# A copy on ScalarE between the values' bank and VectorE's transposition, and one order for all slots, in a fused two-layer cross-attention kernel

## The chip, the cores and the metric

The kernel runs on one core of a Trainium2 chip. The metric is device time in microseconds (us) of one execution; lower is better. The engines are called as the profile calls them: PE is TensorE's matmul, PEld its weight load, DVE is VectorE, ACT is ScalarE, POOL is GpSimd, SP is SyncE, which issues most of the DMAs.

## The reference, cut to what matters

Two cross-attention layers follow each other. x has 32 batches of 256 rows and 320 channels; each batch has a context of 77 rows of 512 channels. There are 20 heads of 16 channels. In the first layer the context is cut into the text (77 rows) and three further parts, which are empty here, since there are 77 rows in all; the same holds for the second layer. What is left in each layer is

```
q = heads(x @ Wq);  k = heads(ctx @ Wk);  v = heads(ctx @ Wv)     # 20 heads of 16
s = q @ k^T / sqrt(16)                                            # 256 x 77 for each head
p = softmax(s);  o = merge(p @ v)
x = o @ Wo + bias + x                                             # input of the next layer
```

All of it is float32.

## The kernel before, in words

x stands turned in SBUF, channels on the partitions. Two batches are handled together, as a pair; a **unit** is one pair in one layer, so there are 16 pairs x 2 layers = 32 units. The 40 (batch, head) products of a unit are worked in five **groups**, g = 0 to 4, each with four pairs of heads side by side in the four 32-row or 32-column tiles of PE's array.

For a group the steps are these.

- `maxima` (L491 on): PE computes the scores once in float32 into four PSUM banks (`psm`, L500), and DVE takes the maximum of each row (L512). `turn` (DVE, then DMAs) brings a unit's maxima into the place where the scores step reads them.
- `scores` (L545 on): PE computes the scores turned, keys on the partitions, into four banks (`pss`): first minus the maximum (L550), then the product from split halves (L558). ACT takes four exponentials of 77x512 (L564, tile `pT`).
- `products` (L566 on, called by `values`): PE multiplies with the values, and with a column of ones for the sums, into one bank `po` of 128x512 (L578).
- `divide` (L587, called by `values`): DVE turns the bank in 32x32 blocks into SBUF (`turned`, L590) and takes the reciprocal of the sums (`inv`, L594); POOL multiplies (`normal`, L599).
- `turn_back` (L610): DVE turns `normal` back into the unit's output tile `oT` (L613).

When all five groups of a unit are in `oT`, `outputs_and_queries` (L388) multiplies with Wo (`psy`) and, interleaved with it, makes the queries of another unit (`psq`). Within it `main_channels` and `rest_main` read groups 0 to 3 of `oT`; `last_channels` and `rest_last` read group 4, and they come behind. Then DVE adds bias and residual (`x`, L620) and ACT copies the queries out of PSUM (L418, L421). `keys` makes `psk` (ACT copies it, POOL masks it), `vals` makes `psv` (ACT copies it into a stage, DMAs place it).

PSUM is one pool of eight banks; `po`, `pss`, `psm`, `psk`, `psv`, `psy` and `psq` all draw from it in turn, so that the bank that a step wants next is the one taken eight allocations ago.

The order of all instructions is written out by hand (`tc.manual_schedule()`): each engine runs its instructions in the order in which the program issues them. The main loop at the end walks over **slots**; `at(slot, where, step)` puts a step into a slot, and within a slot the steps go by their `where`. Slots from -10 to 0 start the kernel, slots 1 to 134 carry the units. `slot_of` gives the slot of a group's scores; its values come one slot later, and its `turn_back` two slots later (`"turn back"`), for g = 4 at the end of the values' own slot (`"back"`).

Before the change a slot is called heavy when the columns put down for it with `at(..., columns)` exceed 10 x 256, and two orders are in use:

```
        if slot > 0 and work_of[slot] > 10 * S:
            order = ("load", "scores", "turn back", "maxima") + rest
        else:
            order = ("load", "maxima", "turn back", "scores") + rest
```

with rest = ("values", "rest", "back", "turn", "split", "full", "last"). In every slot the values come behind the scores.

A unit takes four slots (or five where its number is a multiple of 4). The first of them is the large one: the scores of groups 0 and 1 (eight exponentials; in units 4, 8, ..., 28 only group 0, four exponentials, and a step of maxima), the values of the unit before's group 4, its `"back"`, and `outputs_and_queries` of the unit before. Then come slots of 3.5 to 6.2 us with one group's scores, one step of maxima, one or two groups' values, and some of keys and vals.

Of the kernel before, what the change touches and what calls it, by code (L numbers as in the profile page):

```python
# [59 lines left out]
HEADS, HD = 20, 16  # L60
# [35 lines left out]
def xattn_kernel(ctx: ExitStack, tc: tile.TileContext, xT, cT, cP, weights, outT):  # L96
# [24 lines left out]

    def load_context(u):
        p = units[u][0]
        c_sb = cs[u] = io.tile([P, NKA, NB * L], F32, tag="c", name=f"c_{u}", bufs=3)
        nc.sync.dma_start(out=c_sb, in_=cP[:, p])


# [23 lines left out]

    ones = const.tile([P, P], F32, name="ones")
    nc.vector.memset(ones, 1.0)
    ident = const.tile([P, P], F32, name="ident")
    make_identity(nc, ident)


# [160 lines left out]
    def keys(u, t):  # L318
        p, layer = units[u]
        w, c_sb = w_sb[layer], cs[u]  # L320
        if t == 0:
            st[u]["kr"] = work.tile([P, NG, L], F32, tag="kR", name=f"kR_{u}", bufs=2)
        kR = st[u]["kr"]
        ps = bank(f"psk_{u}_{t}")
        for kc in range(NKA):
            by_columns(
                ps[:, 0 : 2 * L],
                w["k"][:, kc, t * P : (t + 1) * P],
                c_sb[:, kc, :],
                start=(kc == 0),  # L330
                stop=(kc == NKA - 1),
            )
        nc.scalar.copy(kR[:, 2 * t : 2 * t + 2].rearrange("p g k -> p (g k)"), ps[:, 0 : 2 * L])
        mask_keys(u, t)

    def keys_rest(u):

        p, layer = units[u]
        w, c_sb = w_sb[layer], cs[u]
        ps = bank(f"psk_{u}_2")  # L340
        for kc in range(NKA):
            for i in range(4):
                b, m = 1 - i // 2, i % 2
                nc.tensor.matmul(  # L344
                    ps[32 * i : 32 * i + 32, 0:L],
                    w["k"][:, kc, 2 * P + 32 * m : 2 * P + 32 * m + 32],
                    c_sb[:, kc, b * L : (b + 1) * L],
                    start=(kc == 0),
                    stop=(kc == NKA - 1),
                )  # L350
        nc.scalar.copy(st[u]["kr"][:, 4], ps[:, 0:L])
        mask_keys(u, 2)
# [35 lines left out]
    def outputs_and_queries(u, uq):  # L388

        w, wq, o, x = w_sb[units[u][1]], w_sb[units[uq][1]], st[u]["o"], xs[units[uq][0]]  # L390
        q0 = new_queries(uq)
        y = [[bank(f"psy_{u}_{t}_{b}") for b in range(NB)] for t in range(2)]
        main_channels(y, w["o"], o, start=True, stop=False)
        y2 = bank(f"psy_{u}_2")
        rest_main(y2, w["o"], o, start=True, stop=False)


        q2 = bank(f"psq_{uq}_2")
        q = [[bank(f"psq_{uq}_{t}_{b}") for b in range(NB)] for t in range(2)]
# [12 lines left out]
        for g in range(4):  # L412
            add(u, g, y[g // 2][g % 2])
        add(u, 4, y2)
        store(u)

        rest_main(q2, wq["q"], x, start=False, stop=True, swap=1)
        nc.scalar.copy(of_group(q0, 4), q2[:, 0:S])  # L418
        main_channels(q, wq["q"], x, start=False, stop=True)
        for g in range(4):  # L420
            nc.scalar.copy(of_group(q0, g), q[g // 2][g % 2][:, 0:S])  # L421
# [165 lines left out]
    def divide(u, g, po):  # L587

        turned = work.tile([P, 2 * (S + HD)], F32, tag="turned", name=f"turned_{u}_{g}", bufs=2)
        nc.vector.transpose(turned[:, 0 : 2 * S], po)  # L590

        sums = turned[:, HD : 2 * S - HD].rearrange("p (e n) -> p e n", e=2)[:, :, 0 : S - HD : 32]
        inv = work.tile([P, 2, S // 32], F32, tag="inv", name=f"inv_{u}_{g}", bufs=2)
        nc.vector.reciprocal(inv, sums)  # L594

        outs = turned.rearrange("p (e n) -> p e n", e=2)[:, :, 0:S]
        outs = outs.rearrange("p e (q r) -> p e q r", r=32)[:, :, :, 0:HD]
        normal = work.tile([P, S // 32, 2, HD], F32, tag="normal", name=f"normal_{u}_{g}", bufs=2)
        nc.gpsimd.tensor_tensor(  # L599
            normal.rearrange("p q e d -> p e q d"),  # L600
            outs,
            inv.unsqueeze(3).broadcast_to([P, 2, S // 32, HD]),
            ALU.mult,
        )
        return normal
# [47 lines left out]

    place = {}

    work_of = {}

    def at(slot, where, step, columns=0):

        place.setdefault((slot, where), []).append(step)  # L660
        work_of[slot] = work_of.get(slot, 0) + columns

    def start(u):

# [18 lines left out]
    for u, (p, layer) in enumerate(units):  # L683

        s = start(u - 2)
        if layer == 0 and u > 0:
            at(s - 5 - (u == 1), "load", lambda p=p: load_x(p))
        if u > 0:
            at(s - 4, "load", lambda u=u: load_context(u))
        if u > 1:  # L690
            k = (0, 1, 2) if u == 2 else (s - 2, s - 1, s + 1)
            at(k[0], "rest", lambda u=u: keys(u, 0), 8 * 2 * L)
            at(k[1], "rest", lambda u=u: keys(u, 1), 8 * 2 * L)
            at(k[2], "rest", lambda u=u: keys_rest(u), 8 * L)
        paired = u > 2 and u - 3 not in late
        if paired:
            at(s, "full", lambda u=u: outputs_and_queries(u - 3, u), 50 * S)
        elif u > 1:
            at(s, "last", lambda u=u: queries(u), 25 * S)
        if u > 1:  # L700
            at(s + 2, "split", lambda u=u: split_keys(u))
            at(start(u - 1), "load", lambda u=u: spread_keys(u))
            for i in range(3):
                at(start(u - 1) + i - 1, "split", lambda u=u, i=i: split_queries(u, i))
                at(start(u - 1) + i, "load", lambda u=u, i=i: spread_queries(u, i))
        need = range(p * NB * L // P, ((p + 1) * NB * L - 1) // P + 1)
        new = [i for i in need if i >= made[layer]]
        made[layer] += len(new)
        first = (-6, -2)[u] if u < 2 else start(u - 1) + 1
        slots = {}  # L710
        for k, i in enumerate(new):
            at(first - 3 - (u == 0) + k, "load", lambda layer=layer, i=i: load_chunk(layer, i))
            if i in few:
                slots[i] = first
                at(first, "full", lambda layer=layer, i=i: vals_of_few(layer, i), 8 * 96)
                continue
            for h in range(2):
                slots[i] = first + (0 if u < 2 else k if len(new) > 1 else h)
                at(slots[i], "full", lambda layer=layer, i=i, h=h: vals(layer, i, h), 4 * C)
        for i in need:  # L720
            at(slots.get(i, first), "full", lambda u=u, i=i: place_vals(u, i))
        for g in range(NG):
            slot = slot_of(u, g)
            at(slot, "scores", lambda u=u, g=g: scores(u, g))
            at(slot + 1, "values", lambda u=u, g=g: values(u, g), 4 * S)
            if g < 4:
                at(slot + 2, "turn back", lambda u=u, g=g: turn_back(u, g))
            else:
                at(slot + 1, "back", lambda u=u, g=g: turn_back(u, g))
        if u == NU - 1:  # L730
            at(end, "full", lambda u=u: finish(u), 20 * S)
            at(end, "last", lambda u=u: finish_rest(u))
        if u in late:
            for t in range(2):
                at(late[u][t], "full", lambda u=u, t=t: finish(u, (t,)), 10 * S)
            at(late[u][2], "rest", lambda u=u: finish_rest(u), 5 * S)
            at(max(late[u]), "last", lambda u=u: store(u))


# [59 lines left out]

    rest = ("values", "rest", "back", "turn", "split", "full", "last")  # L800
    for slot in range(min(s for s, _ in place), max(s for s, _ in place) + 1):
        if slot > 0 and work_of[slot] > 10 * S:
            order = ("load", "scores", "turn back", "maxima") + rest
        else:
            order = ("load", "maxima", "turn back", "scores") + rest
        for where in order:
            for step in place.get((slot, where), ()):
                step()
# [98 lines left out]
```

## Time and profile before

| what | value |
|---|---|
| median of 3 runs (lowest to highest) | 938.5 us (937.83 to 941.53) |
| profiled execution, its own time | 937.7 us |
| its span in the profile | 935.9 us |
| granted TensorE clock | 0.999 |
| PE busy | 924.1 us, 99% of the span |
| PEld busy | 634.5 us, 68% |
| DVE busy | 572.4 us, 61% |
| ACT busy | 435.9 us, 47% |
| POOL busy | 413.6 us, 44% |

The profiled execution's own time lies 1.8 us above its span and 0.8 us below the median of the runs. Busy shares are of the whole span; a matmul's end is modelled, and matmuls overlap, so a busy PE is not a PE without waits: the waits are seen in how long a slot takes from its first matmul to the next slot's first.

### The profile page before, as it was taken

Reading aid. Unit: us, or ns where it says so; the run is one execution under the profiler, and the core shown is the slowest. Engines: PE = TensorE matmul, PEld = TensorE weight load, DVE = VectorE, ACT = ScalarE, POOL = GpSimd, SP = SyncE. Lnnn points to the kernel's source line nnn. Section 1 sums busy time; section 2 is a strip of 40 time slices with the busy share of each in tenths; the row PEclk is TensorE's granted clock in tenths of the full one; section 3 lists DMA queues with packets and bytes.
Section 4 is the critical chain, followed back from the end, with each engine's and each line's share of the span. In section 5 each row is a group of like instructions: output and inputs, shape, how many; then the busy total and the mean of one; then the engine's idle time right before and its main releaser. Section 6 shows DMA issues by size and latency. Waiting matters only on the chain.

```text
span 935.9 us, 48848 instructions
## 1 busy us (share of the span) xinstructions
PE 924.1 (99%) x21582; PEld 634.5 (68%) x21582; DVE 572.4 (61%) x1324; ACT 435.9 (47%) x975; POOL 413.6 (44%) x614
## 2 busy tenths in 40 slices
PE   9999999999999999999999999999999999999998
PEld 7667766777666777666766667766677766676654
DVE  4485656656566665656556566665467554776575
ACT  2355443554435553454534545434454445444562
POOL 4464334543345543345434455343554335553431
PEclk9999999999999999999999999999999999999999
DMA  6675245352453624545145452354434543344342
GB/s 242 218 225 163 84 132 171 96 191 81 150 178 103 203 67 148 165 142 189 52 140 171 125 184 82 123 171 162 160 95 118 165 158 115 94 141 126 119 137 98
DMA packets 114740, 133.03 MB, mean 142 GB/s; under 512 B 47012, under 2 KB 76004, under 8 KB 114530
## 3 DMA queue, kind: packets, MB, share of 16 engines
q1 hardware_dynamic: 113666, 127.42, 42.8%
q8 instruction: 170, 2.79, 1.3%
q10 hardware_dynamic: 864, 2.49, 0.7%
q14 instruction: 40, 0.33, 0.1%
HBM read 35.39 MB, written 10.49 MB: 49 GB/s over the span
## 4 chain that ended last, share of the span: by engine, by line
PE 88%; DVE 8%; DMA 2%; issue 1%; SPq 0%; POOL 0%; ACT 0%; ACTq 0%; POOLq 0%
PE psq L203 15%; PE psy L203 15%; PE po L578 14%; PE psm L500 8%; PE pss L558 8%; PE psv L203 7%; PE psk L203 6%; PE pss L550 5%; DVE m L512 4%; PE psy L237 4%; PE psq L237 4%; DVE turned L590 2%; PE psk L344 1%; DVE maxes L533 1%; DMA qs<-halves 1%
## 5 line engine op out<-in xcount | busy, mean ns | idle before, releaser
L564 ACT ACTIVATE pT<-pss 77x512 f32<-77x512 f32 x640 | 327.3, 594 | 125.9 <-PE pss L558 120.1
L512 DVE TENSOR_REDUCE m<-psm 128x6 f32<-128x462 f32 (+2 forms) x512 | 247.4, 549 | 208.6 <-PE psm L500 208.1
L599 POOL TENSOR_TENSOR normal<-turned,inv 128x256 f32<-128x256 f32 x160 | 99.5, 622 | 472.5 <-DVE inv L594 452.8
L578 PE MATMUL po<-pT,v 77*32 77x256 f32 x2560 | 165.9, 384 | 4.7 <-DVE m L512 2.7
L203 PE MATMUL psy<-oT,w 128*32 128x256 f32 (+1 forms) x3072 | 164.4, 379 | 0.0
L203 PE MATMUL psq<-x,w 128*32 128x256 f32 (+1 forms) x3072 | 155.6, 380 | 0.5 <-DMA w<-in_w_dram 0.3
L203 PEld LDWEIGHTS psy<-oT,w 128*32 128x32 f32 (+1 forms) x3072 | 88.3, 108 | 63.4 <-issue 14.4
L590 DVE STREAM_TRANSPOSE turned<-po 128x512 f32<-128x512 f32 x160 | 110.3, 689 | 25.6 <-PE po L578 25.5
L203 PEld LDWEIGHTS psq<-x,w 128*32 128x32 f32 (+1 forms) x3072 | 86.0, 109 | 57.7 <-DVE x L620 4.5
L274 POOL TENSOR_SCALAR kT<-kR,masks 128x154 f32<-128x154 f32 x186 | 113.6, 621 | 0.0
L578 PEld LDWEIGHTS po<-pT,v 77*32 77x32 f32 x2560 | 69.6, 109 | 63.4 <-ACT pT L564 18.6
L279 POOL TENSOR_TENSOR halves<-q,halves 128x512 fp32r<-128x512 f32 (+1 forms) x96 | 106.9, 1114 | 8.0
L500 PE MATMUL psm<-kT,q 32*128 32x154 f32 x2560 | 109.4, 296 | 0.0
L558 PE MATMUL pss<-qs,kS 32*77 32x256 f32 x2560 | 106.3, 275 | 0.0
L613 DVE STREAM_TRANSPOSE oT<-normal 128x256 f32<-128x256 f32 x160 | 67.4, 429 | 55.9 <-POOL normal L599 55.9
L620 DVE SCALAR_TENSOR_TENSOR x<-psy,w,x 128x256 f32<-128x256 f32 x160 | 68.4, 476 | 50.7 <-PE psy L203 49.4
L500 PEld LDWEIGHTS psm<-kT,q 32*128 32x128 f32 x2560 | 90.6, 183 | 12.9 <-issue 9.7
L558 PEld LDWEIGHTS pss<-qs,kS 32*77 32x77 f32 x2560 | 88.9, 141 | 10.9
L203 PE MATMUL psv<-w,cv 128*32 128x160 f32 x2432 | 93.2, 299 | 0.2 <-DVE m L512 0.2
L418 ACT COPY q<-psq 128x256 f32<-128x256 f32 x28 | 10.4, 372 | 169.6 <-PE psq L237 169.6
L550 PE MATMUL pss<-max_rows,less 32*77 32x512 f32 x640 | 80.5, 451 | 1.6 <-ACT stage L442 1.6
L203 PEld LDWEIGHTS psv<-w,cv 128*32 128x32 f32 x2432 | 76.8, 110 | 5.2 <-DVE m L512 0.7
(46 smaller groups left out, 725.1 us busy)
## 6 DMA issues: line engine op xcount, KB each, us to landing
qs<-halves SPq DMA_DIRECT2D x256, 128.0 KB
kS<-k_halves SPq DMA_DIRECT2D x128, 192.5 KB
c<-in_cP_dram SPq DMA_DIRECT2D x32, 308.0 KB
cv<-in_cT_dram SPq DMA_DIRECT2D x38, 256.0 KB
out_dram<-x SPq DMA_DIRECT2D x15, 640.0 KB
x<-in_xT_dram SPq DMA_DIRECT2D x14, 640.0 KB
qs<-halves SPq DMA_DIRECT2D x128, 64.0 KB
v<-stage SPq DMA_DIRECT2D x26, 192.5 KB
```

The source lines that it names most:

```text
L203: nc.tensor.matmul(out[m : m + 32], lhsT[:, m : m + 32], rhs, **flags)
L237: nc.tensor.matmul(ps[o : o + 32, 0:S], lhsT, rhs, **flags)
L274: engine.tensor_scalar_mul(kT[:, e], kR[:, groups], masks[:, e : e + 1])
L279: engine.tensor_tensor(low, x, high.bitcast(F32), ALU.subtract)
L500: nc.tensor.matmul(ps[j][:, i * 2 * L : (i + 1) * 2 * L], q[r, c * P : (c + 1) * P], kT[r, :, g % 2, :], start=True, stop=True,)
L512: nc.vector.tensor_reduce(st[u]["m"].rearrange("p e h j -> p h e j")[:, first : first + n, :, j], ps[j][:, at * 2 * L : (at + n) * 2 * L]. ...
L550: nc.tensor.matmul(ps[j][:L], less[r, g % 4, :], max_rows[u % 2][r, g // 4], start=True, stop=False)
L558: nc.tensor.matmul(ps[j][:L, e * S : (e + 1) * S], st[u]["ks"][r, e, g, half, :], q[r, :], start=False, stop=(half == 1 and e == 1),)
L564: nc.scalar.activation(st[u]["p", g][j][:L], ps[j][:L], AF.Exp, scale=SCALE)
L578: nc.tensor.matmul(po[o : o + 32, e * S : (e + 1) * S], vpad[:L, b, pair, e].rearrange("p a d -> p (a d)"), pT[j][:L, e * S : (e + 1) * S] ...
L590: nc.vector.transpose(turned[:, 0 : 2 * S], po)
L599: nc.gpsimd.tensor_tensor(normal.rearrange("p q e d -> p e q d"), outs, inv.unsqueeze(3).broadcast_to([P, 2, S // 32, HD]), ALU.mult,)
```

## The change

Three things change.

- In `divide`, ACT copies the bank `po` (128x512) into a new SBUF tile `whole`, and DVE turns `whole` instead of the bank. `normal` no longer has a tile of its own; it is written over the first half of `whole`.
- To make room, the context tile `c` has two buffers instead of three, and the identity matrix lies in a buffer of `turned`.
- The columns given to `at` and the sum `work_of` are gone; every slot behind slot 0 has the order with the scores ahead and the maxima behind `"turn back"`.

```diff
     def load_context(u):
-        c_sb = cs[u] = io.tile([P, NKA, NB * L], F32, tag="c", name=f"c_{u}", bufs=3)
+        c_sb = cs[u] = io.tile([P, NKA, NB * L], F32, tag="c", name=f"c_{u}", bufs=2)
...
-    ident = const.tile([P, P], F32, name="ident")
+    ident = work.tile([P, 2 * (S + HD)], F32, tag="turned", name="ident", bufs=2)[:, 0:P]
...
     def divide(u, g, po):
 
         turned = work.tile([P, 2 * (S + HD)], F32, tag="turned", name=f"turned_{u}_{g}", bufs=2)
-        nc.vector.transpose(turned[:, 0 : 2 * S], po)
+        whole = work.tile([P, 2 * S], F32, tag="whole", name=f"whole_{u}_{g}", bufs=2)
+        nc.scalar.copy(whole, po)
+        nc.vector.transpose(turned[:, 0 : 2 * S], whole)
...
-        normal = work.tile([P, S // 32, 2, HD], F32, tag="normal", name=f"normal_{u}_{g}", bufs=2)
+        normal = whole[:, 0:S].rearrange("p (q e d) -> p q e d", e=2, d=HD)
...
-    work_of = {}
-
-    def at(slot, where, step, columns=0):
-
+    def at(slot, where, step):
         place.setdefault((slot, where), []).append(step)
-        work_of[slot] = work_of.get(slot, 0) + columns
...
     for slot in range(min(s for s, _ in place), max(s for s, _ in place) + 1):
-        if slot > 0 and work_of[slot] > 10 * S:
+        if slot > 0:
             order = ("load", "scores", "turn back", "maxima") + rest
         else:
             order = ("load", "maxima", "turn back", "scores") + rest
```

More of the change, by code (lines that the diff above doesn't have):

```diff
@@ L691, in xattn_kernel @@
             k = (0, 1, 2) if u == 2 else (s - 2, s - 1, s + 1)
-            at(k[0], "rest", lambda u=u: keys(u, 0), 8 * 2 * L)
-            at(k[1], "rest", lambda u=u: keys(u, 1), 8 * 2 * L)
-            at(k[2], "rest", lambda u=u: keys_rest(u), 8 * L)
+            at(k[0], "rest", lambda u=u: keys(u, 0))
+            at(k[1], "rest", lambda u=u: keys(u, 1))
+            at(k[2], "rest", lambda u=u: keys_rest(u))
         paired = u > 2 and u - 3 not in late
         if paired:
-            at(s, "full", lambda u=u: outputs_and_queries(u - 3, u), 50 * S)
+            at(s, "full", lambda u=u: outputs_and_queries(u - 3, u))
         elif u > 1:
-            at(s, "last", lambda u=u: queries(u), 25 * S)
+            at(s, "last", lambda u=u: queries(u))
         if u > 1:
@@ L714, in xattn_kernel @@
                 slots[i] = first
-                at(first, "full", lambda layer=layer, i=i: vals_of_few(layer, i), 8 * 96)
+                at(first, "full", lambda layer=layer, i=i: vals_of_few(layer, i))
                 continue
@@ L718, in xattn_kernel @@
                 slots[i] = first + (0 if u < 2 else k if len(new) > 1 else h)
-                at(slots[i], "full", lambda layer=layer, i=i, h=h: vals(layer, i, h), 4 * C)
+                at(slots[i], "full", lambda layer=layer, i=i, h=h: vals(layer, i, h))
         for i in need:
@@ L724, in xattn_kernel @@
             at(slot, "scores", lambda u=u, g=g: scores(u, g))
-            at(slot + 1, "values", lambda u=u, g=g: values(u, g), 4 * S)
+            at(slot + 1, "values", lambda u=u, g=g: values(u, g))
             if g < 4:
@@ L730, in xattn_kernel @@
         if u == NU - 1:
-            at(end, "full", lambda u=u: finish(u), 20 * S)
+            at(end, "full", lambda u=u: finish(u))
             at(end, "last", lambda u=u: finish_rest(u))
@@ L734, in xattn_kernel @@
             for t in range(2):
-                at(late[u][t], "full", lambda u=u, t=t: finish(u, (t,)), 10 * S)
-            at(late[u][2], "rest", lambda u=u: finish_rest(u), 5 * S)
+                at(late[u][t], "full", lambda u=u, t=t: finish(u, (t,)))
+            at(late[u][2], "rest", lambda u=u: finish_rest(u))
             at(max(late[u]), "last", lambda u=u: store(u))
```

## Prediction, made before the change was run

> **What bounds the kernel now.** I read the page's busy times, its shares of the chain that ended last, its groups of instructions, and then the timeline slot by slot. The lines below are one of each of the first two and three groups (busy time, mean ns of one; idle time before them and who ended it).
>
> ```profile
> PE 924.1 (99%) x21582; PEld 634.5 (68%) x21582; DVE 572.4 (61%) x1324; ACT 435.9 (47%) x975; POOL 413.6 (44%) x614
> ...
> PE 88%; DVE 8%; DMA 2%; issue 1%; SPq 0%; POOL 0%; ACT 0%; ACTq 0%; POOLq 0%
> ...
> L564 ACT ACTIVATE pT<-pss 77x512 f32<-77x512 f32 x640 | 327.3, 594 | 125.9 <-PE pss L558 120.1
> ...
> L590 DVE STREAM_TRANSPOSE turned<-po 128x512 f32<-128x512 f32 x160 | 110.3, 689 | 25.6 <-PE po L578 25.5
> ...
> L613 DVE STREAM_TRANSPOSE oT<-normal 128x256 f32<-128x256 f32 x160 | 67.4, 429 | 55.9 <-POOL normal L599 55.9
> ```
>
> PE is the bound: 99% busy, and 88% of the chain that ended last is its own work; the rest of the chain is mostly DVE (8%), which gives banks back late. ACT, which takes on the copy, is 47% busy on average. But an average says nothing of a slot, and PE waits in a few places only, so I measured slots in the timeline, from PE's first matmul in one to its first in the next; the program's order tells which matmuls are whose.
>
> There are three kinds that matter. **Large double slots** (scores of two groups, then the values of group 4 of the unit before, then that unit's output): 21 with an output step (the first slots of units 1 to 28 that are not multiples of 4), 13.75 us each. **Large single slots** (units 4, 8, ..., 28): 7, at 14.3 to 14.4 us, one at 13.76. **Light slots**, the ones whose order changes: some 45.
>
> This is a double slot, slot 30, from 232.86 on (timeline: start, duration, what, and in brackets the idle time before it):
>
> ```profile
> 233.88 3.98 ACT L564 ACTIVATE pT<-pss 77x512 f32<-77x512 f32 x8 [0.60 <-PE pss L558]
> ...
> 235.69 0.72 DVE L590 STREAM_TRANSPOSE turned<-po 128x512 f32<-128x512 f32 x1 [0.93 <-PE po L578]
> ...
> 238.16 0.45 DVE L613 STREAM_TRANSPOSE oT<-normal 128x256 f32<-128x256 f32 x1 [1.47 <-POOL normal L599]
> ...
> 239.85 0.42 PE L203 MATMUL psy<-oT,w 64*32 64x256 f32 x4
> ```
>
> Read it from the last line: the 64-row matmuls of `last_channels` are the first to need group 4 of `oT`. It is back at 238.61, PE comes for it at 239.85: 1.24 us to spare. DVE took the bank at 235.69, while ACT was in the middle of its eight exponentials, which end at 237.86.
>
> **The copy, in the double slots.** ACT runs in program order, and the scores of a slot stand ahead of its values, so the copy of `po` comes behind all eight exponentials. Its length: ACT's copies out of PSUM take 225 ns for 77 columns and 372 for 256 (groups L351 and L418), 0.82 ns a column, so about 0.58 us for 512; the exponential of 512 columns at 594 ns is the nearest row. Eight exponentials in 3.98 us overlap by 0.11 each; a copy that does the same ends at 238.34, one that does not at 238.44. From there the path back to `oT` is the old one without waits, as a single slot (34, from 260.69) shows it in the timeline:
>
> ```profile
> 264.68 0.70 DVE L590 STREAM_TRANSPOSE turned<-po 128x512 f32<-128x512 f32 x1
> ...
> 266.40 0.45 DVE L613 STREAM_TRANSPOSE oT<-normal 128x256 f32<-128x256 f32 x1 [0.73 <-POOL normal L599]
> ...
> 267.67 0.42 PE L203 MATMUL psy<-oT,w 64*32 64x256 f32 x4
> ```
>
> 264.68 to 266.85 is 2.17 us. With some 0.05 us for each of two handovers, `oT` reaches PE at 240.6 to 240.7 where PE comes at 239.85: a new wait of 0.76 to 0.86 us; I take 0.80. POOL is free by then (its `halves` end before 238.1). PE has nothing else in order to do and is the bound, so all of it counts: 21 x 0.80 = **+16.8 us**. Bounds for one copy: 0.37 us (the 256-column row) makes it 0.59, or 12.4 in all; 0.69 (DVE's own 512-column read of the bank) makes it 0.91, or 19.1. Behind PE, the five `x` additions, the queries' copies and their banks move with it.
>
> **The copy elsewhere.** In slots with one group's scores ACT is done after four exponentials, about 3.06 us into the slot, when DVE is still in its maxima (to 4.03 us): the copy (160 x 0.58 = 93 us in all, ACT to 57%) lies beside them and costs nothing; without that cover it would cost what it does above. It gives the bank back earlier than DVE does, worth nothing unless PE waits for it. In the last slots (130 to 133) ACT has eight exponentials and two copies for slots of 4.8 to 7.3 us; banks come late once, and I put +1.0 there (0 to 2).
>
> DVE's transposition now reads SBUF. The rows say this costs the same: 689 ns for 512 columns from PSUM, 429 for 256 from SBUF, so 1.02 ns a column with equal overhead. [...]
>
> **The order, in light slots.** Scores first, PE no longer waits for banks that DVE's `turned` holds. What such a slot takes without waits: the heavy slot ahead of it has the same work and one `psv` of 32 matmuls more, takes 4.80, and that block takes 1.09 in the chain of work in order of time: 3.71. Light slots third in their unit take 3.84 (12 of them) or 4.12 (7); those of units 4, 8, ... gain 0.12 (5) or 0.04 (14) by the same count. One (slot 113, 5.59 us, PE held by late maxima) I put at -0.9; slots 50 and 63 wait for a DMA of `v` and keep that; slots 1 to 4 at zero, since DVE has no room there. 12 x 0.13 + 7 x 0.41 + 1.2 + 0.9 = **-6.5 us** (3 to 10).
>
> But `turn_back` now stands ahead of the maxima, and DVE has to wait for POOL:
>
> ```profile
> 230.09 2.21 DVE L512 TENSOR_REDUCE m<-psm 128x6 f32<-128x462 f32 x4
> 230.26 0.62 POOL L599 TENSOR_TENSOR normal<-turned,inv 128x256 f32<-128x256 f32 x1 [2.59 <-DVE inv L594]
> ...
> 232.22 0.43 DVE L613 STREAM_TRANSPOSE oT<-normal 128x256 f32<-128x256 f32 x1
> ```
>
> In this light slot (29, from 228.73 to 232.86, timeline) the maxima run while POOL works. Afterwards `oT` waits until 230.9, ends at 231.35, and the maxima run to 233.6 instead of 232.3: 1.3 later, in a slot that ends 0.4 earlier. Ahead of a double slot this is swallowed, as DVE is idle there until the copy ends. Ahead of a single slot DVE enters about 1.7 late, with maxima of its own to do: its `turned` moves from 3.99 us into the slot to about 5.5, `oT` from 6.16 to 7.7 where PE comes at 6.98, and behind it `turn` and the `x` additions, for which the query banks wait already, come 1.5 later. That is 3 x 1.5 (slots 34, 85, 119) and 1.2 for slot 102; where the light slot ahead was a 3.84 one (17, 51, 68), 0.6 each. Sum **+7.5 us**, from 0 (all absorbed) to 10.5 (7 x 1.5).
>
> **Buffers.** `c` with two: its load stands four slots ahead of the unit's query slot, and the keys that read the buffer's old content are at least three slots back; SP's queue is not held. `whole` is rewritten two groups later, when its `turn_back` is past on DVE. `ident` is read once at the start. All zero; if a load of `c` did wait, what stands behind it on SP is the next `qs` and `v` transfers.
>
> **Sum** against the profiled execution: 937.7 + 16.8 + 1.0 - 6.5 + 7.5 = 956.5, and with the 0.8 us by which the median lies above it, 957.
>
> **Rivals.** (1) *Faster.* The copy gets to ACT early enough, the banks come back sooner, and the light slots' gain is all that is left: 938.5 - 6.5 = 932. It decides at one point: a copy that ends by about 237.5 in the double slot above, 0.9 us sooner than I reckon, before the eighth exponential is over. The order of issue speaks against it. 0.07. (2) *Only the copy costs*, DVE catches up in the single slots: 938.5 + 17.8 - 6.5 = 950. 0.25. (3) *DVE becomes the bound in rows of light slots*: a light slot's DVE work with the wait for POOL is 0.45 + 2.24 + 0.69 + 0.25 + 0.75 = 4.4 us against PE's 3.71; if the spare banks do not cover that in the 14 or so light slots that stand second or later in a row, at most +0.7 each, about 10: 967. The banks (eight, about ten allocations a slot) speak against it for runs of three. 0.15. (4) *It cancels*: copies at the short bound (12.4), light slots at 10, nothing else: 941. 0.05. The forecast itself: 0.48.
>
> Half a percent (about 4.7 us) is what a measurement of this kernel can tell from no change. Faster by more: rival 1, 0.07; within: rival 4, 0.05; slower: the rest, 0.88. The range leaves out rivals 1 and 4 and the end of rival 3: 946 to 967. Forecast, 2 and 3 are all slower; alone, the forecast's own bounds are 950 to 963.
>
> **What would show it.** In a double slot: the copy starting where the eighth exponential ends (about 5.0 us into the slot), `turned` behind it at 5.5 instead of 2.83, PE waiting 0.8 us for DVE `oT` ahead of the 64-row `psy`, the slot at 14.55 instead of 13.75. Light slots at 3.7. ACT busy near 530 us. In single slots 34, 85 and 119, `turned` at about 5.5 us and the slot near 15.9. I am wrong if the copy lands between exponentials, if `last_channels` does not wait, or if double slots stay at 13.75.

## The result, and the profile after

The changed kernel takes 970.7 us (median of 4 runs, 965.8 to 972.2) where the kernel before takes 940.0 beside it (4 runs, 937.8 to 941.6): 1.032 times as long, 95% interval 1.029 to 1.035. The forecast was 957, range 946 to 967. The direction was right, the size was not: 13.7 us too low, and the time lies 3.7 us outside the range. The profiled execution of after took 965.8 us, with a span of 964.0.

The page of after, in the parts that the prediction read of before (busy times; shares of the chain that ended last; groups with busy time, mean ns of one, and idle time ahead with who ended it):

```profile
PE 934.9 (97%) x21582; PEld 643.3 (67%) x21582; DVE 577.1 (60%) x1324; ACT 510.2 (53%) x1135; POOL 416.2 (43%) x614
...
PEclk9999999999999999999999999999999999999989
...
PE 71%; DVE 11%; ACT 8%; DMA 3%; POOL 3%; issue 2%; SPq 1%; ACTq 0%; POOLq 0%
...
L564 ACT ACTIVATE pT<-pss 77x512 f32<-77x512 f32 x640 | 326.8, 594 | 88.5 <-PE pss L558 78.8
...
L592 DVE STREAM_TRANSPOSE turned<-whole 128x512 f32<-128x512 f32 x160 | 110.8, 692 | 72.5 <-ACT whole L591 72.5
...
L615 DVE STREAM_TRANSPOSE oT<-whole 128x256 f32<-128x256 f32 x160 | 68.3, 435 | 80.5 <-POOL whole L601 80.3
...
L591 ACT COPY whole<-po 128x512 f32<-128x512 f32 x160 | 91.8, 592 | 5.8 <-DVE oT L615 3.0
```

The copy takes 592 ns. DVE's transposition, now from SBUF, takes 692 ns where it took 689 from the bank, and its 72.5 us of idle time ahead are now all for ACT. ACT, at 0% of the chain before, has 8% of it. And in the 39th of the 40 slices the clock that PE was granted (the row PEclk, in tenths) is down to 8. In before's page the same row reads

```profile
PEclk9999999999999999999999999999999999999999
```

and nothing in the prediction speaks of the clock.

The double slot again, in the timeline of after: slot 30, which starts at 236.43.

```profile
237.39 3.98 ACT L564 ACTIVATE pT<-pss 77x512 f32<-77x512 f32 x8 [0.54 <-PE pss L558]
...
241.22 0.62 ACT L591 COPY whole<-po 128x512 f32<-128x512 f32 x1
241.87 0.71 DVE L592 STREAM_TRANSPOSE turned<-whole 128x512 f32<-128x512 f32 x1 [2.20 <-ACT whole L591]
...
243.67 0.45 DVE L615 STREAM_TRANSPOSE oT<-whole 128x256 f32<-128x256 f32 x1 [0.80 <-POOL whole L601]
244.17 0.13 PEld L203 LDWEIGHTS psy<-oT,w 64*32 64x32 f32 x5 [0.83 <-DVE oT L615]
```

The copy starts 4.79 us into the slot, behind the eighth exponential, DVE turns it at 5.44, and PE's loads for the 64-row `psy` sit 0.83 us idle until `oT` is there. Before, PE came 1.24 us after `oT`. The slot takes 14.5 us instead of 13.75. This is the forecast's picture.

The single slot 34, from 264.72:

```profile
267.88 2.24 DVE L512 TENSOR_REDUCE m<-psm 128x6 f32<-128x462 f32 x4
268.00 0.59 ACT L591 COPY whole<-po 128x512 f32<-128x512 f32 x1 [0.26 <-PE po L578]
...
270.04 0.69 DVE L592 STREAM_TRANSPOSE turned<-whole 128x512 f32<-128x512 f32 x1
...
272.32 0.13 PEld L203 LDWEIGHTS psy<-oT,w 64*32 64x32 f32 x5 [0.56 <-DVE oT L615]
```

Here the copy is early and lies free in SBUF for 1.4 us, because DVE is still in its maxima: `turned` starts 5.3 us into the slot (5.5 was forecast, 3.99 before) and the slot takes 15.8.

The forecast is furthest off in the last slots, above all in slot 131, from 929.11, where ACT has eight exponentials and two copies:

```profile
929.49 1.08 ACT L591 COPY whole<-po 128x512 f32<-128x512 f32 x2
...
929.89 1.19 PE L550 MATMUL pss<-max_rows,less 32*77 32x512 f32 x3
930.12 0.71 DVE L592 STREAM_TRANSPOSE turned<-whole 128x512 f32<-128x512 f32 x1 [4.56 <-ACT whole L591]
...
931.04 0.65 DVE L592 STREAM_TRANSPOSE turned<-whole 128x512 f32<-128x512 f32 x1
...
931.90 0.40 DVE L622 SCALAR_TENSOR_TENSOR x<-psy,w,x 128x256 f32<-128x256 f32 x1
...
932.35 0.45 PE L550 MATMUL pss<-max_rows,less 32*77 32x512 f32 x1 [1.27 <-DVE x L622]
```

Two copies of `po` stand behind exponentials on ACT; the transpositions stand behind the copies; an `x` addition stands behind the transpositions on DVE; and the bank that this addition frees is the one that PE needs for `pss`, for which it sits idle for 1.27 us. In before (slot 131 from 907.17) the four `pss` matmuls that take these banks come together:

```profile
907.92 0.41 PE L550 MATMUL pss<-max_rows,less 32*77 32x512 f32 x4
```

There the last of them has started by 0.8 us into the slot; in after it starts at 3.24. So late banks cost some 2.4 us here, more than the idle time shows, because the second and third of the four wait for a bank as well. The windows around it (start:end, length, then the busy time of PE, PEld, DVE, ACT and POOL, the granted clock, DMA share, GB/s) show what came of that:

```profile
923.00:929.00 6.00, 6.00 (x136) 3.87 (x124) 2.13 (x5) 3.99 (x9) 1.70 (x3) 1.00 0.52 166
929.00:931.00 2.00, 1.97 (x27) 1.09 (x23) 0.84 (x2) 2.00 (x6) 0.00 (x0) 1.00 0.50 185
931.00:933.00 2.00, 0.73 (x17) 0.65 (x17) 1.83 (x6) 1.04 (x3) 1.24 (x2) 1.00 0.49 149
933.00:937.00 4.00, 4.00 (x46) 1.69 (x49) 0.23 (x1) 1.89 (x4) 0.00 (x0) 0.54 0.18 51
937.00:940.50 3.50, 3.50 (x48) 1.30 (x32) 1.79 (x4) 1.59 (x4) 0.98 (x2) 0.55 0.11 37
940.50:946.00 5.50, 5.50 (x104) 3.24 (x96) 1.55 (x4) 3.51 (x8) 0.26 (x1) 1.00 0.31 120
```

PE was busy for 0.73 of 2.0 us, and right behind that its clock stood near a half for about 7 us, in which it has 12 to 14 matmuls to the microsecond instead of 23. (A window of 933.4 to 940.1 alone shows 0.50; the ones up to 933.3 and from 940.2 on show 1.00.) It counts as busy all the while, so the busy times hide it; the clock column does not. At 0.54 and 0.55, these two windows hold, by estimate, 4 x 0.46 + 3.5 x 0.45 = 3.4 us of lost clock. Slot 131 takes 11.67 us instead of 5.98. Slots 129, 130 and 132 are 0.2, 0.4 and 0.5 us longer at full clock.

Slot by slot (PE's first matmul to the next slot's first, in the two profiles), the 28.1 us between the spans lie here:

| part | forecast | measured |
|---|---|---|
| 21 double slots | +16.8 | +16.9 |
| 7 single slots | +7.5 | +8.8 |
| light and heavy slots, the first four | −6.5 | −3.7 |
| last slots, 128 to 134 | +1.0 | +6.8 |
| ahead of slot 1 | 0 | −0.7 |
| sum against before's profile | +18.8 | +28.1 |
| median above the profiled execution | +0.8 | +4.9 |

The last row is the second surprise. The profiled execution of after is its fastest run; the other three took 970.4 to 972.2. Of the 13.7 us that were missed, 9.3 are in the profile and 4.1 in this row (the rest is rounding).

### The profile page after: what moved, and what is told of

Its sections match the earlier page's. It is cut to its first block, busy times and chain, and to the rows that moved or that the text cites. A ratio compares the mean times of both kernels' runs of the same rounds, so it can differ in the third digit from the quotient of the medians.

```text
span 964.0 us, 48905 instructions
## 1 busy us (share of the span) xinstructions
PE 934.9 (97%) x21582; PEld 643.3 (67%) x21582; DVE 577.1 (60%) x1324; ACT 510.2 (53%) x1135; POOL 416.2 (43%) x614
## 4 chain that ended last, share of the span: by engine, by line
PE 71%; DVE 11%; ACT 8%; DMA 3%; POOL 3%; issue 2%; SPq 1%; ACTq 0%; POOLq 0%
PE psq L203 15%; PE po L578 12%; PE psv L203 8%; PE pss L558 7%; ACT pT L564 7%; PE psm L500 7%; PE pss L550 6%; PE psk L203 6%; PE psy L203 5%; DVE m L512 4%; PE psq L237 4%; DVE turned L592 3%; POOL whole L601 2%; DMA v<-stage 2%; DVE oT L615 2%
## 5 line engine op out<-in xcount | busy, mean ns | idle before, releaser
L601 POOL TENSOR_TENSOR whole<-turned,inv 128x256 f32<-128x256 f32 x160 | 101.9, 637 | 504.0 <-DVE inv L596 445.7
L203 PE MATMUL psy<-oT,w 128*32 128x256 f32 (+1 forms) x3072 | 167.1, 383 | 13.0 <-DVE oT L615 12.7
L592 DVE STREAM_TRANSPOSE turned<-whole 128x512 f32<-128x512 f32 x160 | 110.8, 692 | 72.5 <-ACT whole L591 72.5
L203 PEld LDWEIGHTS psy<-oT,w 128*32 128x32 f32 (+1 forms) x3072 | 90.9, 109 | 79.1 <-DVE oT L615 26.2
L615 DVE STREAM_TRANSPOSE oT<-whole 128x256 f32<-128x256 f32 x160 | 68.3, 435 | 80.5 <-POOL whole L601 80.3
L500 PEld LDWEIGHTS psm<-kT,q 32*128 32x128 f32 x2560 | 94.4, 183 | 4.3 <-DVE m L512 1.6
L591 ACT COPY whole<-po 128x512 f32<-128x512 f32 x160 | 91.8, 592 | 5.8 <-DVE oT L615 3.0
```

The costliest lines, as they stand in the source:

```text
L203: nc.tensor.matmul(out[m : m + 32], lhsT[:, m : m + 32], rhs, **flags)
L500: nc.tensor.matmul(ps[j][:, i * 2 * L : (i + 1) * 2 * L], q[r, c * P : (c + 1) * P], kT[r, :, g % 2, :], start=True, stop=True,)
L591: nc.scalar.copy(whole, po)
L592: nc.vector.transpose(turned[:, 0 : 2 * S], whole)
L601: nc.gpsimd.tensor_tensor(normal.rearrange("p q e d -> p e q d"), outs, inv.unsqueeze(3).broadcast_to([P, 2, S // 32, HD]), ALU.mult,)
```

## The experiments

The theory after the result was that the prediction's mechanism holds in the double slots and that the rest of the miss is PE's clock, lost in slot 131 and, in most runs, somewhere else. Its rivals were that the copy costs by its mere length, and that the new order makes DVE the bound. Each ratio is to the kernel before on the same chip (medians 941.2 to 941.7), with its 95% interval; slot figures compare profiles with before's.

### Each part by itself

The copy alone (with the smaller buffers), in the order of before:

```diff
-        nc.vector.transpose(turned[:, 0 : 2 * S], po)
+        whole = work.tile([P, 2 * S], F32, tag="whole", name=f"whole_{u}_{g}", bufs=2)
+        nc.scalar.copy(whole, po)
+        nc.vector.transpose(turned[:, 0 : 2 * S], whole)
```

> The copy on ACT, the two smaller buffers and nothing else: the order of the slots is that of before. Theory 1 (the copy behind eight exponentials makes PE wait for oT in the 21 double slots, and in the last slots it makes a wait so long that PE's clock falls): double slots at 14.5 us, single slots as before (14.4), slot 131 at about 11.7 us with a granted clock of about 0.7 around it; span 935.9 + 16.9 + 6.9 = about 959 us. Theory 2 (the order is what costs, by DVE's late maxima and late banks; the copy is hidden): double slots at 13.8, span 936 to 942. Theory 3 (copy and order cost only together): as theory 2.

Measured: 975.2 us, 1.038 (1.033 to 1.042), so the copy alone costs more than the whole change. Double slots +17.3, single ones +4.4, the last slots +7.7 (131: +5.6), and light slots +8.8, where the forecast put nothing for the copy. With the maxima first, the exponentials of a light slot end later (in slot 29 at 3.84 us instead of 3.01 in after) and the copy is behind them; DVE's transposition, and the next maxima on DVE, come later with it. In slot 37, which loses 0.4, PE sits idle for 0.26 us until DVE is done with a bank of maxima. That the copy "lies beside them and costs nothing" held only under the new order. But half of the +8.8 is slot 63 (+4.2), where PE waits 2.6 us for a DMA (the section on the last slots has this wait) and the clock falls as in slot 131 (windows of this kernel, columns as above):

```profile
479.00:486.00 7.00, 7.00 (x90) 4.73 (x94) 1.41 (x3) 2.97 (x7) 1.58 (x3) 0.51 0.38 117
```

The order alone, on the kernel before:

```diff
-        if slot > 0 and work_of[slot] > 10 * S:
+        if slot > 0:
```

> Scores ahead in every slot behind the first, and nothing else: DVE turns the bank itself as before. Theory 1: double slots at 13.75 us, single slots at about 15.7 where the slot ahead is a light one with late maxima (+8.8 in all), light and heavy slots 4 us shorter in sum, the end as before; span 935.9 + 8.8 - 4 = about 941 us, less than 1% over before. Theory 2: span above 955 us. Theory 3: span at or below 936.

Measured: 954.0 us, 1.015 (1.011 to 1.019), with a span of 947.9 where I had expected 941. Double slots +4.3, single ones +4.0, light ones +2.9 instead of a gain. So scores ahead of maxima isn't a gain that the copy spoils: without the copy it is a loss. In span, copy alone is +39.4 and order alone +12.0; together they are +28.1 (some 5 us of the +39.4 are the wait and the clock in slots 63 and 64). Their times in slot 29 fit that they help each other: the order lets ACT start its copy at 2.9 us instead of 3.7, and the copy is done with the bank at 3.5, where with the order alone DVE turns the bank, behind its maxima, from 4.7 to 5.4.

### The double slots

The copy left out in slots that hold the scores of two groups (DVE reads the bank there):

```diff
+        if [slot_of(w, h) for w in range(NU) for h in range(NG)].count(slot_of(u, g) + 1) > 1:
+            nc.vector.transpose(turned[:, 0 : 2 * S], po)
+        else:
             nc.scalar.copy(whole, po)
             nc.vector.transpose(turned[:, 0 : 2 * S], whole)
```

> The changed kernel, but in the slots in which ACT has eight exponentials (the double slots and 129 to 132) DVE turns the bank itself; everywhere else ACT copies. Theory 1: double slots back to 13.75 us, slot 131 back to 6 us, granted clock 0.999, span 964.0 - 17 - 7 = about 940 us. Theory 2: the copy is not the cause, span within 3 us of 964. Theory 3 (reading the bank late anywhere holds PE's banks up): about half of the loss stays, 950.

Measured: 948.6 us, 1.011 (1.007 to 1.016). Double slots +1.9 in all instead of +16.9, and the last slots, which this edit also changes, +0.3 instead of +6.8. Single slots stay at +8.8, light ones at −2.8. The copy in these slots is the cause of both.

Is it the copy's length or its place? The copy kept, but in the double slots the values of group 4 put between the scores of the two groups:

```diff
+        if 0 < slot < 124 and len(place.get((slot, "scores"), ())) > 1:
+            place[slot, "back"] = place[slot, "scores"][1:] + place[slot, "back"]
+            place[slot, "scores"] = place[slot, "scores"][:1]
```

> The changed kernel, but in the double slots the values of group 4 stand between the two groups' scores, so that the copy is fourth, not eighth, behind exponentials; the copy itself stays. Theory 1 (what PE waits for is the copy's place in ACT's queue): copy at about 3.0 us into the slot, oT back at 5.8, the 64-row psy at 7.0, double slots at 13.75; span 964.0 - 16.9 = about 947 us. Rival (the longer way of the data itself, one operation more, is what PE feels): double slots stay above 14.2 us, span 957 or more.

Measured: 953.4 us, 1.012 (1.010 to 1.015). Slot 30 of this kernel, from 233.65, in the timeline:

```profile
236.53 0.59 ACT L591 COPY whole<-po 128x512 f32<-128x512 f32 x1
237.00 2.08 ACT L564 ACTIVATE pT<-pss 77x512 f32<-77x512 f32 x4
237.16 0.71 DVE L592 STREAM_TRANSPOSE turned<-whole 128x512 f32<-128x512 f32 x1 [0.26 <-ACT whole L591]
...
240.31 0.45 DVE L615 STREAM_TRANSPOSE oT<-whole 128x256 f32<-128x256 f32 x1 [2.15 <-POOL whole L601]
```

The copy starts 2.88 us into the slot instead of 4.79, and two thirds of the loss are gone (+5.3 in the 21 slots). A copy of the same length, behind four exponentials instead of eight: its place is what costs. What remains, about 0.25 a slot, may be POOL, for which DVE waits 2.15 us in the last line while POOL works on `halves`; that was not tried, and the order alone also has +4.3 in these slots. The span of this profile, 958.8, is on the rival's side of what was expected, but not by the double slots: it has +9.4 in the last slots, where the clock falls behind a wait of 2.2 us in slot 132, and +2.9 in slot 63.

### The last slots and the clock

The copy left out from slot 128 on, the rest as in after:

```diff
+        if slot_of(u, g) + 1 >= 128:
+            nc.vector.transpose(turned[:, 0 : 2 * S], po)
+        else:
             nc.scalar.copy(whole, po)
             nc.vector.transpose(turned[:, 0 : 2 * S], whole)
```

> The changed kernel, but from slot 128 on DVE turns the bank itself. Theory 1: slot 131 back to about 6 us, granted clock from 0.996 to 0.999, span about 957, and the runs lie closer together than the changed kernel's (965.8 to 972.2). Rival: the clock falls because of the many waits of 0.8 us in the double slots, and the last slots only show it: clock stays at 0.996 or lower, span 962 or more.

Measured: 962.7 us, 1.024 (1.021 to 1.028), 8.0 us below after. The last slots are at +0.1. So the copies bring about the wait in slot 131, and the fall of the clock with it. The span, 959.6, is above the 957 expected, and two of the four runs have a clock of 0.996, so this is not the whole. The same profile shows a second place where the clock falls, slot 63, which after's profile doesn't have (timeline, then windows):

```profile
472.85 0.49 ACT L442 COPY stage<-psv 128x160 f32<-128x160 f32 x2 [5.47 <-DMA v<-stage]
473.20 1.02 PEld L500 LDWEIGHTS psm<-kT,q 32*128 32x128 f32 x20 [3.12 <-ACT stage L442]
473.20 1.25 PE L500 MATMUL psm<-kT,q 32*128 32x154 f32 x20 [2.88 <-ACT stage L442]
```

```profile
469.00:473.00 4.00, 1.32 (x32) 0.88 (x24) 0.45 (x1) 0.15 (x1) 2.97 (x5) 1.00 0.32 76
473.00:475.00 2.00, 1.80 (x32) 1.43 (x36) 0.76 (x2) 2.00 (x6) 0.00 (x0) 1.00 0.33 108
475.00:478.50 3.50, 3.50 (x55) 2.36 (x48) 2.67 (x6) 1.15 (x3) 0.91 (x2) 0.51 0.48 149
```

ACT waits for the DMAs that empty a stage buffer, PE waits 2.88 us for ACT's copy of `psv`, and then PE has half its clock. Before has the wait too ("slots 50 and 63 wait for a DMA of `v` and keep that", as the prediction says), but a shorter one, and the clock in its profile stays up (timeline, then windows):

```profile
461.61 0.65 PE L550 MATMUL pss<-max_rows,less 32*77 32x512 f32 x2 [0.92 <-ACT stage L442]
```

```profile
459.00:462.00 3.00, 2.08 (x49) 1.39 (x43) 1.51 (x3) 0.49 (x2) 2.91 (x5) 1.00 0.33 79
462.00:466.00 4.00, 4.00 (x102) 3.06 (x101) 2.53 (x6) 2.60 (x6) 1.31 (x3) 1.00 0.33 99
```

How long the wait is differs from profile to profile: ACT's copy into the stage waits 3.56 us for the DMAs in before and 5.47 in this kernel. PE sits idle in slot 63 for 0.5 to 0.9 us in five profiles (before, after, the order alone, the copy left out in double slots, and the reordering of the next section), all with the clock up, and for 2.4 to 2.9 us in four (the copy alone, the values in between, this one, and the old order ahead of single slots), all with the clock down behind it.

If this wait is where the runs beside the profiled one lose their time, taking it away must bring the median down to the profile. The DMAs of the older stages are issued at the end of the slot ahead, so that ACT finds the buffer free, in after and in before:

```diff
-            at(slots.get(i, first), "full", lambda u=u, i=i: place_vals(u, i))
+            if u > 2 and i not in slots:
+                at(first - 1, "last", lambda u=u, i=i: place_vals(u, i))
+            else:
+                at(slots.get(i, first), "full", lambda u=u, i=i: place_vals(u, i))
```

On after:

> The changed kernel, but the DMAs that place values of an older stage are issued at the end of the slot ahead, the large one, so that ACT's copy into the stage does not wait for them in slots 49 and 62. Theory (the runs of this kernel spread because slots 50 and 63 wait for that landing, and in some runs long enough for PE's clock to fall): slots 50 and 63 at about 3.8 us instead of 4.8 and 5.0, granted clock no lower than 0.995, the median 3 to 6 us below 970.7 and within 2 us of its own profiled execution. Rival (the spread comes from elsewhere, such as the last slots): only the profile gets 2 us shorter, the median stays 4 to 5 us above it.

Measured: 965.8 us, 1.026 (1.023 to 1.028), 4.9 us below after, and now 0.5 us from its own profiled execution (965.3). Slots 50 and 63 are 1.2 and 1.6 us shorter than before's; the last slots stay at +7.3, and with them clocks from 0.993 to 0.998 in the four runs.

On before:

> The kernel before, and only the DMAs that place values of an older stage are issued at the end of the large slot ahead. Theory (runs of the kernel before also lose PE's clock now and then, by the wait of ACT's stage copy for that landing in slots 49 and 62): slots 50 and 63 at 3.8 us instead of 4.9 and 5.3, granted clock 0.998 or more in every run, runs within 2 us of each other, median 934 to 937. Rival (the spread of before has another cause): profile 2 us shorter, the runs still spread over 4 us with clocks of 0.996.

Measured: 935.3 us, 0.995 (0.993 to 0.997). Seven of nine runs, all with a granted clock of 1.0, lie within 934.5 and 935.7; the other two, at 0.998, took 937.8 and 939.3. The 14 runs of before in this comparison range from 936.4 to 944.0: the nine at a clock of 0.994 to 0.996 took 939.3 and more, the three at 0.999 or 1.0 took 938.2 or less; the two at 0.998 took 938.2 and 941.4. So before lost some 4 us in most of its runs, and its profiled execution (937.7, clock 0.999) was one of those that did not. That they lose it in this place follows from what the early DMAs take away; no profile of such a run of before was kept.

Both edits on after, the tail without copies and the early DMAs:

> The changed kernel with DVE turning the bank itself from slot 128 on and the older stage placed early: the two waits are gone after which PE's clock fell. Theory: what is left are the terms of the prediction alone, double slots +17, single slots +9, light and heavy slots -5 to -7; granted clock 0.998 or more in every run, median 954 to 958. Rival (the clock falls from the many waits of 0.8 us as well): clocks of 0.996 and less stay, median above 960.

Measured: 957.2 us, 1.018 (1.015 to 1.022). The three runs beside the profiled one took 956.9 to 957.4, at clocks of 0.999 to 1.0. This is the forecast's number, but in part by chance, since these DMAs help before as well: against before with the same early DMAs (935.3) it is 21.9 us slower, where the forecast without its tail term makes 17.8. Between the profiles of these two, the double slots have +16.9, the single ones +8.1, the light and heavy ones −3.6, the first four +3.4 and the last ones +0.1: what is missing from the forecast then is mostly the light slots' gain. The profiled run of this kernel (960.7) loses its clock in yet another place, in slot 3, where its windows show 0.59 and 0.56 from 54 to 62 us.

### The single slots, and light slots in the old order

If `turn_back`'s wait for POOL is what delays DVE, maxima ahead of it must keep the order's gain without its loss. On the kernel before, light slots with scores, maxima, turn back:

```diff
+            if slot > 0:
+                order = ("load", "scores", "maxima", "turn back") + rest
```

> The kernel before, but light slots have scores, maxima, turn back: scores ahead of maxima as in the change, while turn back stays behind the maxima; DVE turns the bank itself. Theory 1 (what costs in the new order is that DVE waits for POOL ahead of the maxima, not that the scores go first): single slots within 0.2 us of 14.4, double slots at 13.75, light slots 0.1 to 0.3 us shorter; span 930 to 935, against 947.9 of the order alone. Rival (scores first itself delays the maxima and so the banks): span 942 or more, single slots over 14.8.

Measured: 955.2 us, 1.015 (1.012 to 1.018), no better than the order alone; the span is 951.6, and I had expected 930 to 935. So here the wait for POOL is not what costs. Slot 29, from 233.31, in the timeline:

```profile
235.39 2.28 DVE L512 TENSOR_REDUCE m<-psm 128x6 f32<-128x462 f32 x4 [0.64 <-PE psm L500]
...
237.94 0.67 DVE L590 STREAM_TRANSPOSE turned<-po 128x512 f32<-128x512 f32 x1
```

With the scores first, PE reaches the `psm` matmuls later, DVE's maxima start 2.08 us into the slot instead of 1.36, and DVE's `turned` comes at 4.6, behind the end of a slot of 4.25 us, instead of at 3.84 in one of 4.13: where DVE itself holds the bank, that bank comes back late. Single slots +4.3, double ones +6.3.

The other way round, the old order in the seven light slots ahead of a single one (with the tail without copies):

```diff
-        if slot > 0:
+        if slot > 0 and slot not in (16, 33, 50, 67, 84, 101, 118):
```

> The changed kernel, DVE turning the bank itself from slot 128 on, and in the seven light slots ahead of the single slots the order is that of before (maxima, turn back, scores). Theory (half of the single slots' loss is maxima that begin later, the other half the copy, which in the old order comes later still): single slots 34, 85 and 119 at about 15.0 us, between before's 14.4 and the changed kernel's 15.8, +4 to +5 in all seven. Rival (the new order alone is the cause): 14.4 us, +0 to +1 in all.

Measured in a single run: 963.8 us, at a clock of 0.995 (slots 3 and 63 have +4.2 and +3.2 in it). What it was for shows in the slots: single ones +4.8 instead of +8.8, with 34, 85 and 119 at 15.0 us instead of 15.8. (With the new order there and the same tail they have +7.5.) So the order of the light slot ahead makes about half of the loss of these three; the prediction had put all of it there. What is left is about what the copy by itself makes in the old order (+4.4), by the late transpositions described above.

### What can be kept

The copy only in slots with the scores of one group, light slots with scores, maxima, turn back, and the early DMAs:

```diff
+        if [slot_of(w, h) for w in range(NU) for h in range(NG)].count(slot_of(u, g) + 1) > 1:
+            nc.vector.transpose(turned[:, 0 : 2 * S], po)
+        else:
+            nc.scalar.copy(whole, po)
+            nc.vector.transpose(turned[:, 0 : 2 * S], whole)
...
+            if slot > 0:
+                order = ("load", "scores", "maxima", "turn back") + rest
```

> A version made of the parts that should pay: ACT copies only where one group's scores stand in the slot, DVE turns the bank itself elsewhere; light slots have scores, maxima, turn back; the older stage is placed early. Theory 1: no new waits in the double and the single slots, light slots at 3.7, slots 50 and 63 at 3.8; span 926 to 931, median 0.7 to 1.2% below before. Rival (the copy on ACT costs in the light slots too): span 936 or more.

Measured: 937.2 us, 0.996 (0.994 to 0.998). Light and heavy slots gain 6.4, double ones 0.8, single ones lose 7.1. That is no better than before with the early DMAs alone (0.995).

Last, the new order only in the 14 light slots ahead of a double one, and the copy only there and in heavy slots with one group, up to slot 123:

```diff
+        if groups == 1 and slot < 124 and (work_of[slot] > 10 * S or slot in ahead_of_double):
+            nc.scalar.copy(whole, po)
+            nc.vector.transpose(turned[:, 0 : 2 * S], whole)
+        else:
+            nc.vector.transpose(turned[:, 0 : 2 * S], po)
...
+    ahead_of_double = [start(w) - 1 for w in range(2, 28) if w % 4 > 1]
...
+            if slot in ahead_of_double:
+                order = ("load", "scores", "maxima", "turn back") + rest
```

> Scores first, then maxima, then turn back, in the fourteen light slots that come right ahead of a double slot as the third of their unit, the old order in all other light slots; ACT copies in those fourteen and in heavy slots with one group's scores, DVE turns the bank itself elsewhere; the older stage is placed early. Theory: light slots -2, heavy -1.7, double -0.8, slots 50 and 63 -2.7 against before, single slots and the end as before; span about 929 us, median 930 to 932, about 1% below before. Rival (the gains of light slots are given back in the slot behind): span 932 to 934, as the kernel before with early placing.

Measured: 934.5 us, 0.993 (0.990 to 0.996), the fastest of all, though 930 to 932 was expected: the first slots lose 2.1 us and single ones 2.1, and in its profile the clock falls twice for 3.4 us, from 51.9 and from 799.5. The early DMAs alone make 0.995 (0.993 to 0.997) of before, and the intervals overlap; what copy and order add to that is not told apart from nothing.

## Why the prediction was right and wrong

**Right: the double slots.** 21 x 0.80 was +16.8, and it is +16.9. The working holds line by line: copy behind the eighth exponential (4.79 us into the slot), 0.59 long for 0.58, `turned` at 5.44 for 5.5, PE idle for `oT`. Both counter-experiments agree: without the copy all but 1.9 us of the loss is gone, with an earlier copy two thirds of it. Rival 1 (a copy that is early enough) is out.

**Right in kind, short in size: the single slots**, +8.8 for +7.5. Slots 34, 85 and 119 were put at 1.5 and lost 1.4, with `turned` and the `x` additions as late as forecast. Slots 17, 51 and 68 were put at 0.6 each and lost 0.6, 0.4 and 1.4 (the light slot ahead of 51, slot 50, took 4.94 us in before, and not 3.84 as the prediction has it). Slot 102 was put at 1.2 and lost 2.2; it is 1.0 longer with the early DMAs on before as well, so much of that is before's profile. Rival 2 (DVE catches up there) is out.

**Too good: the light slots**, −3.7 with the heavy ones for −6.5. Third light slots came down to 3.71, as forecast, in eight of the twelve of one set, but only to 3.83 in the other. Those that stand second or later in a row, put at a gain of 0.04 each, lost 0.15 to 0.18 with one exception: rival 3 by its place, at a quarter of the 0.7 that it was priced at; that DVE is the cause was not tested. Slot 113 gained 1.9, for the 0.9 forecast, and its neighbour 114 gave 1.4 of that back. The 1.5 that heavy slots gained was forecast at nothing, and need not come from the change: the early DMAs alone, without copy or new order, gain as much there (1.5, most of it in slots 24, 66, 75 and 95, which gain the same in after). And the reason for the gain ("PE no longer waits for banks that DVE's `turned` holds") was incomplete: the order alone, with DVE still holding the bank, is a loss.

**The first step that failed** is the one for the last slots: "banks come late once, and I put +1.0 there (0 to 2)". A late bank was seen, but not how late and how often, nor what follows. Banks come late in four slots and not once, for some 3.5 us in all: 2.4 in slot 131 and 0.2 to 0.5 in each of slots 129, 130 and 132. And behind the longest of these waits PE has half its clock for 6.8 us, which by the estimate above is another 3.4. The term measured +6.8, and +0.1 without the copies there.

**The second** is "the 0.8 us by which the median lies above" the profiled execution, carried over from before to after. That number was a property of three runs and not of the kernel: the profiled run of before had a short wait for `v<-stage` and kept its clock, where by their clocks most runs did not, and with after the median lies 4.9 above. Taking that wait away closes the gap to 0.5. That the prediction let slots 50 and 63 "keep that" was right for the profile and wrong for the median.

No term and no rival of the prediction had the clock in it, and it has a share in both failed steps. Before's page gave no sign of it (a clock of 0.999, no digit under 9). Its three runs gave one: 937.8, 938.5 and 941.5 is a spread about which the prediction did not ask.

**Right: the transposition from SBUF.** The prediction put it at the same cost as from PSUM, by before's rows for 512 and 256 columns. The transposition of 512 columns took 692 ns from SBUF and 689 from the bank: the rows were right to follow.

## What to carry to other kernels

What an evacuation (emptying a PSUM bank into SBUF) costs on another engine can depend on where it stands in that engine's queue more than on its length: here 592 ns cost 0.8 us a slot behind eight exponentials, about 0.25 behind four. When PE is the bound, ask of every new wait what it does to PE's clock as well as how long it is (in slot 131 a wait of 1.27 us had 6.8 us at half the clock behind it); windows with the clock column show this where the busy time says 97%. And compare the granted clocks of several runs before a profile's own time is taken for the kernel's: here 14 runs of before took 936.4 to 944.0 us at clocks of 0.994 to 1.0, and with earlier DMAs alone seven of nine took 934.5 to 935.7, all at 1.0.

## What the runs showed of the chip

PE's granted clock fell to a half (0.51 to 0.59 in the windows above, 0.50 where a window holds nothing else) for about 3.4 us at a time (475 to 478.5 in the kernel with the tail without copies, at 0.51) or 6.8 (933.4 to 940.1 in after, at 0.50). It did so behind a stretch with PE busy for 0.73 of 2.0 us and a wait of 1.27, and behind one with 1.32 of 4.0 and a wait of 2.88. It did not behind 2.08 of 3.0 us in before's profile, nor behind the 21 waits for `oT` in after's double slots, in which PE sits idle for 0.29 to 0.74 us. Nor did it behind a wait of 1.51 us in before's slot 113, where PE was busy for 0.49 of 2.0 us (800 to 802):

```profile
801.72 1.07 PE L578 MATMUL po<-pT,v 77*32 77x256 f32 x16 [1.51 <-DVE m L512]
```

Over the fourteen profiles, from slot 1 on, a fall stands behind each of the five idle stretches of PE of 2.2 to 2.9 us, behind five of the twelve of 1.2 to 1.9 us, and behind none of 1.0 to 1.14. One and the same wait can go either way: 1.27 us in slot 131 of after had the fall behind it, 1.28 us in the same slot of the kernel with the values in between did not. Twice, in slot 3, the clock fell without a single idle stretch of 1 us.

Which share of idle time in which window decides was not measured, and why slot 3 loses its clock in two of the profiles stays open too.
